# Four-image convolutional network on one core: the input of the tap matrices computed for two chunks of rows at a time, one on each half of TensorE's columns, with the second copy of each half written by VectorE

## The chip, the cores and the metric

The kernel runs on one core of one Trainium2 chip. The metric is the time of one execution on the device, in microseconds (us). Three runs before the change took 1929.0, 1927.67 and 1920.48 us, so the median is 1927.67 us. The profile comes from a further execution whose span is 1934.2 us; TensorE's granted clock was 0.961 of full speed on average in it.

## The reference

The input is a batch of 4 images of 256 channels and 56 x 56 pixels in fp32. Four residual layers follow each other, each on the group-normalised image:

- Layer 0 is an involution: a 1x1 convolution reduces the 256 channels to 64 (`h`), a second one makes from `h` 7 x 7 weights for each pixel and each of 16 groups of channels, and each pixel's 7 x 7 neighbourhood is summed with its own weights.
- Layer 1 is two 3x3 convolutions with batch norm and ReLU.
- Layer 2 is again an involution, with batch norm and ReLU after the first 1x1 convolution and after the sum.
- Layer 3 gates the image by channel and by pixel.

The change concerns the first 1x1 convolution of layers 0 and 2:

```python
h = jnp.einsum('bchw,oc->bohw', xk, reduce_w) + reduce_b[None, :, None, None]          # layer 0
t = jnp.einsum('bchw,oc->bohw', x, w1)
t = jax.nn.relu(_bn_eval(t, bn1_gamma, bn1_beta, bn1_mean, bn1_var))                    # layer 2
```

All is fp32 and stays so.

## The kernel before, in words

`involution_layer` handles layers 0 and 2, `conv_layer` layer 1; layer 3's gates are worked into layer 2. An involution layer goes through 8 units, one for each image `b` and block `cb` of 128 channels. A unit has two stages:

- `tap_matrices` (the tap stage): 32 steps of six matmuls (L436) that multiply `h` with shifted tables `z_sb`. Their results are brought from PSUM to `kt`, in three steps of four by VectorE (L454), in the fourth by ScalarE (L447).
- `apply`, over 7 columns `tx` of the image: 56 small matmuls (L478), of 64 columns and then of 32 columns of the array, multiply `kt` with the windows `xw` of the image. ScalarE (L491 in layer 0, L493 in layer 2) and VectorE (L498, in layer 2 also L505) take the results from PSUM. After the matmuls of each column come `next_windows`, which transposes a strip of the image (L364), copies it to `xw` (L365) and fills the rest of `xw` by DMA (L371, L373) for the column three places on, and `next_strip` (L345 or L347).

The 1x1 convolution is `bottleneck(b)`, a generator that is advanced step by step between other work. Its weights `red_sb` hold the 64 outputs twice, so that a matmul over all 128 columns of the array leaves `h` on partitions 0 to 63 and again on 64 to 127 of `hp`; `tap_matrices` reads both copies, one for each half of the array's rows. The first step scales the weights (`redn`, L384) and clears a corner of `hp` (L386, GpSimd), the second computes the bias `hb` (L391, L400 or L402). Seven further steps handle one chunk of 9 rows each (the last has 2 rows): two matmuls of 504 elements (L408), one for each block of input channels, then three ScalarE instructions (L420 in layer 0, L422 in layer 2) that write the chunk to `hp` in the order in which `tap_matrices` reads it.

All PSUM tiles of these layers come from one pool, `banks`, of four buffers of two banks, used in turn. `hp` has one buffer.

The order of the work is written out by hand: the main loop keeps lists `early[tx]` and `late[tx]` of steps that run ahead of a column's `apply` and after it, and at the end `in_order` ties each engine's instructions to the order in which the program wrote them. The first image's `bottleneck(0)` runs ahead of the first unit. That of image `b + 1` is spread over the columns of unit `(b, 1)`: in layer 0 the steps stand in `late[3]` to `late[5]` and `early[6]`, in layer 2 in `late[0]` to `late[5]` and `early[6]`.

## Time and profile before

| what | value |
|---|---|
| median of 3 runs | 1927.67 us |
| span of the profiled execution | 1934.2 us |
| TensorE busy | 1754.1 us, 91% |
| VectorE busy | 1413.4 us, 73% |
| ScalarE busy | 750.9 us, 39% |
| L408, matmuls of `bottleneck` | 224 records, 94.7 us |
| L478, matmuls of `apply` | 12544 records, 381.4 us |
| L436, matmuls of `tap_matrices` | 6144 records, 389.4 us |
| L454, VectorE's part of `kt` | 384 instructions, 357.6 us |

How to read it: the page names engines PE (TensorE matmuls), PEld (TensorE weight loads), DVE (VectorE), ACT (ScalarE), POOL (GpSimd) and SP (SyncE); a q behind an engine's name is its queue. A line such as L408 is a line of the kernel before. A group's row gives the tiles and shapes, the number of instructions, the time in which at least one of them ran, the mean duration of one, and the engine's idle time just before them with what ended it. Matmuls overlap, so a mean duration is longer than the pace at which they follow each other. The chain of work is followed back from the last instruction to what released it; a long share there means that the end waited for that line.

### The profile page before, as it was taken

To read this page: it belongs to the slowest core of one execution; us is meant where nothing else is said; L and a number is where in the kernel's file an instruction comes from. 1 tells how busy PE (TensorE), PEld (TensorE's weight loads), DVE (VectorE), ACT (ScalarE), POOL (GpSimd) and SP (SyncE) were. 2 spreads that over 40 slices of the span, in tenths; PEclk is the share of its full clock that TensorE was granted. 3 is DMA by queue.
4 is the path that set the end of the run, shared out by engine and by line. 5 is a ranking of instruction groups with operands and counts; after the bars stand their busy time and mean duration, and the time that the engine had idled before them with its cause. 6 is when DMAs were issued, how large, how long until landed. Compare 5 with 4: busy or idle time off the path is not lost.

```text
span 1934.2 us, 55654 instructions
## 1 busy us (share of the span) xinstructions
PE 1754.1 (91%) x24054; PEld 1535.3 (79%) x24054; DVE 1413.4 (73%) x2793; ACT 750.9 (39%) x1660; POOL 430.0 (22%) x615
## 2 busy tenths in 40 slices
PE   5999999999929999999999999997999899999876
PEld 4888888878828888988888888884887777878765
DVE  4685767856779978888887978864766666766773
ACT  2345445444422322222122222113656565565532
POOL 2233432334200000000000000000000581680672
PEclk9999999999969999989999999998999999999995
DMA  3544534444350201111111210113533763763651
GB/s 100 153 145 154 154 110 137 152 142 116 99 203 26 74 30 66 57 55 44 51 57 56 71 38 27 34 60 129 164 132 129 205 204 130 224 205 98 176 149 73
DMA packets 66964, 214.15 MB, mean 111 GB/s; under 512 B 13660, under 2 KB 21648, under 8 KB 63392
## 3 DMA queue, kind: packets, MB, share of 16 engines
q1 hardware_dynamic: 44526, 138.37, 22.9%
q0 software_dynamic: 14848, 65.85, 10.5%
q10 hardware_dynamic: 7346, 6.38, 1.1%
q8 instruction: 190, 3.11, 0.7%
q14 instruction: 54, 0.44, 0.1%
HBM read 74.68 MB, written 49.16 MB: 64 GB/s over the span
## 4 chain that ended last, share of the span: by engine, by line
PE 56%; DVE 30%; DMA 5%; issue 4%; POOL 3%; ACT 1%; SPq 1%; ACTq 0%; POOLq 0%; DVEq 0%
PE ps L478 15%; PE mm L1151 12%; DVE kt L454 12%; PE mm L1075 9%; PE ps L436 7%; PE ps L408 5%; PE ps L364 4%; DVE res L1144 3%; PE mm L1047 2%; DMA xw<-xw 2%; DVE un L498 1%; DVE v L1014 1%; PE ps L665 1%; DVE st L1194 1%; PE ps L561 1%
## 5 line engine op out<-in xcount | busy, mean ns | idle before, releaser
L478 PE MATMUL ps<-kt,xw 126*32 126x48 f32 (+1 forms) x12544 | 381.4, 235 | 41.6 <-issue 17.7
L478 PEld LDWEIGHTS ps<-kt,xw 126*32 126x32 f32 (+1 forms) x12544 | 339.8, 121 | 91.8 <-issue 48.8
L454 DVE TENSOR_TENSOR kt<-ps,zb_sb 126x798 f32<-126x798 f32 x384 | 357.6, 978 | 61.7 <-PE ps L436 61.0
L436 PE MATMUL ps<-hp,z_sb 64*126 64x133 f32 x6144 | 389.4, 283 | 12.1 <-DVE kt L454 6.2
L1151 PE MATMUL mm<-v,u_sb 128*128 128x280 f32 (+1 forms) x1728 | 392.6, 388 | 1.3 <-DVE u_sb L877 1.3
L436 PEld LDWEIGHTS ps<-hp,z_sb 64*126 64x126 f32 x6144 | 372.2, 189 | 26.5 <-DVE kt L454 7.4
L1151 PEld LDWEIGHTS mm<-v,u_sb 128*128 128x128 f32 x1728 | 331.0, 192 | 56.6 <-DVE u_sb L877 1.6
L447 ACT ACTIVATE kt<-ps,zb_sb 126x133 f32<-126x133 f32 x768 | 224.1, 441 | 173.4 <-PE ps L436 173.4
L1075 PE MATMUL mm<-v,u_sb 128*128 128x252 f32 (+1 forms) x864 | 192.3, 383 | 0.0
L498 DVE SCALAR_TENSOR_TENSOR un<-ps,par_sb,un 128x240 f32<-128x240 f32 x224 | 98.2, 457 | 123.8 <-ACT un L491 119.3
L498 DVE SCALAR_TENSOR_TENSOR un<-ps,s,un 128x240 f32<-128x240 f32 x224 | 102.4, 457 | 115.3 <-ACT un L493 109.4
L1075 PEld LDWEIGHTS mm<-v,u_sb 128*128 128x128 f32 x864 | 162.6, 189 | 26.1
L1188 POOL DMA_DIRECT2D x<-xr x24 | 13.1, 546 | 704.3 <-DVE xr L1187 704.3
L1047 PE MATMUL mm<-v,u_sb 128*128 128x126 f32 (+1 forms) x864 | 111.2, 281 | 39.2 <-ACT ph L950 30.0
L1047 PEld LDWEIGHTS mm<-v,u_sb 128*128 128x128 f32 x864 | 106.0, 194 | 41.8 <-issue 37.5
L503 POOL TENSOR_TENSOR xs<-un,xs 128x240 f32<-128x240 f32 x112 | 72.2, 664 | 225.5 <-DVE un L498 225.5
L365 ACT COPY xw<-ps 126x896 f32<-126x896 f32 x112 | 101.5, 906 | 48.0 <-PE ps L364 38.7
L1136 ACT ACTIVATE res<-xr,shift,norm_sb 128x1120 f32<-128x1120 f32 (+1 forms) x24 | 30.2, 1260 | 228.8 <-DVE xr L1187 156.2
L364 PE MATMUL ps<-ident_sb,strip_sb 128*126 128x128 f32 x784 | 111.6, 283 | 0.7 <-issue 0.6
L493 ACT ACTIVATE un<-ps,bn_t,s 128x240 f32<-128x240 f32 x112 | 60.2, 538 | 109.0 <-PE ps L478 105.5
L491 ACT ACTIVATE un<-ps,par_sb 128x240 f32<-128x240 f32 x112 | 50.2, 448 | 131.6 <-PE ps L478 129.8
L408 PE MATMUL ps<-xs,redn 128*128 128x504 f32 (+1 forms) x224 | 94.7, 570 | 4.5 <-DMA xs<-x 2.7
(173 smaller groups left out, 1950.8 us busy)
## 6 DMA issues: line engine op xcount, KB each, us to landing
xw<-xw SPq DMA_DIRECT2D x168, 252.0 KB
xw<-xw SPq DMA_DIRECT2D x224, 126.0 KB
xw<-xw POOLq DMA_DIRECT2D x56, 252.0 KB, 4.6
x<-xs POOLq DMA_DIRECT2D x8, 1568.0 KB, 7.8
xs<-in_x_dram SPq DMA_DIRECT2D x6, 1568.0 KB
xs<-x SPq DMA_DIRECT2D x6, 1568.0 KB
x<-xs SPq DMA_DIRECT2D x6, 1568.0 KB
gx<-x POOLq DMA_DIRECT2D x42, 224.0 KB, 6.3
```

The costliest lines, as they stand in the source:

```text
L364: nc.tensor.transpose(ps[:Q, k * P : (k + 1) * P], flat[:, k * Q : (k + 1) * Q], ident_sb)
L365: nc.scalar.copy(xw[:, :NSB, :], ps[:Q, : NSB * P].rearrange("q (n c) -> q n c", n=NSB))
L408: nc.tensor.matmul(ps[:, : rows * W], redn[:, ci].rearrange("p i r -> p (i r)"), xs_of[b, ci][:, j * ROWS_H * W : (j * ROWS_H + rows) * W] ...
L436: nc.tensor.matmul(ps[:Q, i, k * NT : (k + 1) * NT], z_sb[i * R : (i + 1) * R, cb * GB // 2 + gp, z0 : z0 + Q], hp[i * R : (i + 1) * R, py ...
L447: nc.scalar.activation(kt[:, g0 + i, pb, :, k], ps[:Q, i, k * NT : (k + 1) * NT], AF.Identity, bias=zb_sb[:, cb * GB + g0 + i, p0 + k : p0 ...
L454: nc.vector.tensor_tensor(kt[:, g0 : g0 + 2, pb], ps[:Q, :, : PB * NT].rearrange("q i (k t) -> q i t k", k=PB), zb_sb[:, cb * GB + g0 : cb ...
L478: nc.tensor.matmul(v[m * j : m * j + m, i, :, k * TP : (k + 1) * TP], xw[:, window(ty), m * j : m * j + m], kt[:, ng * j : ng * j + ng, :, ...
L498: nc.vector.scalar_tensor_tensor(part, o[e], s, part, ALU.mult, ALU.add)
L503: nc.gpsimd.tensor_tensor(dst, u, dst, ALU.add)
L1047: nc.tensor.matmul(ps[:, co * m : (co + 1) * m], u[ci][:, co * P : (co + 1) * P], v2[:, e, : n // 2, ci * WT : (ci + 1) * WT], start=(ci = ...
L1075: nc.tensor.matmul(ps, u1_sb[:, ci, dy, k, co * P : (co + 1) * P], v[:, k, dy * NB + ci : (dy + n - 1) * NB + ci + 1 : NB, :], start=(j == 0),
L1151: nc.tensor.matmul(ps, u2_sb[:, ci, dy, k, co * P : (co + 1) * P], v[:, k, dy * NB + ci : (dy + n - 1) * NB + ci + 1 : NB, :], start=(j == 0),
```

## The change

`bottleneck` takes two chunks of rows at a time. For each block of input channels it issues two matmuls, each with 64 of the 128 columns of `redn`: the first chunk goes to PSUM partitions 0 to 63, the second to 64 to 127 of one PSUM buffer. So each chunk's `h` comes out once and not twice. ScalarE writes each half to its own partitions of `hp`, with three instructions for each half. The other 64 partitions of each chunk are filled by a VectorE copy from `hp` to `hp` of 24 x 21 elements; the copies of one pair are issued in the step of the next pair, ahead of that step's ScalarE instructions. The layout of `hp` on each partition is as before. The seventh chunk, without a partner, is handled as before.

There are now four chunk steps and not seven, and the lists are adapted: in layer 0 the bias and two pairs run in `late[4]`, the third pair and the short chunk in `late[5]`, nothing in `early[6]`; in layer 2 the bias runs in `late[1]`, the pairs in `late[2]`, `late[3]` and `late[4]`, the short chunk in `late[5]`.

```diff
-                for j in range(NH):
-                    rows = min(ROWS_H, H - j * ROWS_H)
+                weights = [redn[:, ci].rearrange("p i r -> p (i r)") for ci in range(NB)]
+                copies = []
+                for j in range(0, NH, 2):
+                    halves = [slice(0, R), slice(R, P)] if j + 1 < NH else [slice(0, P)]
                     ps = one_bank()
                     for ci in range(NB):
-                        nc.tensor.matmul(
-                            ps[:, : rows * W],
-                            redn[:, ci].rearrange("p i r -> p (i r)"),
-                            xs_of[b, ci][:, j * ROWS_H * W : (j * ROWS_H + rows) * W],
-                            start=(ci == 0),
-                            stop=(ci == NB - 1),
-                        )
...
+                        for i, m in enumerate(halves):
+                            y0 = (j + i) * ROWS_H
+                            rows = min(ROWS_H, H - y0)
+                            nc.tensor.matmul(
+                                ps[m, : rows * W],
+                                weights[ci][:, m],
+                                xs_of[b, ci][:, y0 * W : (y0 + rows) * W],
+                                start=(ci == 0),
+                                stop=(ci == NB - 1),
+                            )
+                    for dst, part in copies:
+                        nc.vector.tensor_copy(dst, part)
+                    copies = []
...
+                    for i, m in enumerate(halves):
+                        rows = min(ROWS_H, H - (j + i) * ROWS_H)
+                        a0, n = (j + i) * ROWS_H // TY, -(-rows // TY)
+                        for py in range(min(rows, TY)):
+                            dst = hp[m, py, :, a0 : a0 + n, :]
+                            if layer == 0:
+                                nc.scalar.activation(dst, s[m, py, :, :n, :], AF.Identity, bias=hb[m])
...
+                        if len(halves) > 1:
+                            part = hp[:, :, :, a0 : a0 + n, :].rearrange("p y x a t -> p (y x) (a t)")
+                            copies.append((part[halves[1 - i]], part[m]))
                     yield
...
-                            late[4] += [step(g)] * 4
+                            late[4] += [step(g)] * 3
                             late[5] += [step(g)] * 3
-                            early[6] += [step(g)] * 2
...
                         late[0].append(step(g))
-                        late[1] += [step(g)] * 2
-                        for tx in range(2, 6):
+                        for tx in range(1, 6):
                             late[tx].append(step(g))
-                        early[6] += [step(g)] * 2
+                        early[6].append(step(g))
```

## The prediction

> **What bounds the kernel now.** I read the page first: the busy shares, then the chain of work that ended last.

> ```profile
> PE 1754.1 (91%) x24054; PEld 1535.3 (79%) x24054; DVE 1413.4 (73%) x2793; ACT 750.9 (39%) x1660; POOL 430.0 (22%) x615
> PE 56%; DVE 30%; DMA 5%; issue 4%; POOL 3%; ACT 1%; SPq 1%; ACTq 0%; POOLq 0%; DVEq 0%
> PE ps L478 15%; PE mm L1151 12%; DVE kt L454 12%; PE mm L1075 9%; PE ps L436 7%; PE ps L408 5%; PE ps L364 4%; DVE res L1144 3%; PE mm L1047 2%; DMA xw<-xw 2%; DVE un L498 1%; DVE v L1014 1%; PE ps L665 1%; DVE st L1194 1%; PE ps L561 1%
> ```

> PE is the bound over most of the span. The line that the change rewrites, L408 (the 1x1 convolution of `bottleneck`), holds 5% of the chain (4.6% where the chain is listed in full, 89 us), and its own busy time is 94.7 us: practically all of it is on the path. Next, the groups with their shapes kept apart, to see what a matmul on half the columns of the array costs here:

> ```profile
> L478 PE MATMUL ps<-kt,xw 126*64 126x96 f32 x4480 | 257.7, 266 | 31.9 <-DVE kt L454 16.0 <-issue 8.3 <-DMA xw<-xw 7.2
> ...
> L408 PE MATMUL ps<-xs,redn 128*128 128x504 f32 x192 | 91.2, 619 | 4.5 <-DMA xs<-x 2.7 <-DVE un L498 1.8
> ...
> L422 ACT ACTIVATE hp<-ps,hb,bn_s 128x168 f32<-128x168 f32 x72 | 30.2, 491 | 33.8 <-PE ps L408 33.8
> ...
> L420 ACT ACTIVATE hp<-ps,hb 128x168 f32<-128x168 f32 x72 | 23.7, 403 | 20.8 <-PE ps L408 20.8
> ```

> Each fp32 matmul leaves two records, its passes (96 matmuls of 504 elements are 192 records). Then the timeline of an image's `bottleneck` in layer 0 and, from the chain of waits over one stage of layer 2, the same work spread over columns:

> ```profile
> 154.94 5.31 PE L408 MATMUL ps<-xs,redn 128*128 128x504 f32 x12 [0.80 <-DVE un L498]
> ...
> 156.91 0.99 ACT L420 ACTIVATE hp<-ps,hb 128x168 f32<-128x168 f32 x3 [2.12 <-PE ps L408]
> ...
> 160.18 3.27 PE L478 MATMUL ps<-kt,xw 126*64 126x96 f32 x112
> ```

> ```profile
> 1425.75 3.22 PE ps L478 x108
> ...
> 1429.88 3.20 PE ps L478 x105
> ...
> 1434.34 1.86 PE ps L408 x4
> 1436.20 3.19 PE ps L478 x103
> ...
> 1440.31 1.69 PE ps L408 x4
> 1442.00 3.23 PE ps L478 x109
> ...
> 1457.75 3.81 PE ps L408 x12
> ```

> The reader is to see three things. A 504-element pass takes 0.422 us (the weight loads of 154.9 to 159.3 us follow one another at that pace; 1.69/4). A column without `bottleneck` takes 4.13 us, one with a chunk 5.82 us, so PE is the pace and the chunk adds its full time. And an image's 28 records cost 10.8 us of PE: 5.31 + 5.50 in layer 0, 1.86 + 3 x 1.69 + 3.81 = 10.74 in layer 2. For the first image of each layer nothing lies beside it:

> ```profile
> 24.12 11.39 PE L408 MATMUL ps<-xs,redn 128*128 128x504 f32 x26
> ...
> 38.18 2.32 PE L436 MATMUL ps<-hp,z_sb 64*126 64x133 f32 x36
> ```

> ```profile
> 1327.05 11.88 PE L408 MATMUL ps<-xs,redn 128*128 128x504 f32 x26 [2.70 <-DMA xs<-x]
> ...
> 1338.54 1.83 ACT L422 ACTIVATE hp<-ps,hb,bn_s 128x168 f32<-128x168 f32 x5 [0.43 <-PE ps L408]
> ...
> 1340.14 2.32 PE L436 MATMUL ps<-hp,z_sb 64*126 64x133 f32 x36 [1.21 <-ACT hp L422]
> ```

> [...] The trace agrees with the overlap: the 64-column group needs 257.7/4480 = 57.5 ns per record, where 96 elements at 0.422/504 us would be 80 ns alone and 40 ns in perfect pairs. [...]

> **The change, part by part.**

> *Matmuls.* Per image 12 long matmuls on 128 columns become 12 on 64 columns, two chunks side by side: 24 passes of 0.422 us (10.14 us) become 12 pair-passes. Perfect pairing gives 5.07 us. For the cost per pass I take L478's excess over perfect pairs, 57.5 - 40 = 17.5 ns a record, 35 ns a pair-pass: 12 x 0.457 = 5.48 us. So 4.66 to 5.07 us saved; I take 4.9. The seventh chunk stays as it was. The order of the matmuls (half 0, half 1, next channel block) alternates the tiles as L478 does. [...]

> *Evictions.* Six of 64 partitions per pair instead of three of 128 per chunk, with as many elements per partition: 20 per image before and after, 0.33 us each in layer 0 (0.99/3), 0.42 in layer 2 (30.2/72). No time saved there, but the pairs now arrive faster than ACT empties them.

> *Copies.* 6 per image, 48 in all, 504 elements. No row shows one[...]. I take 0.42 us: 20 us of DVE work. In the columns DVE does 1.8 us (four L498) and 0.6 us (L807), in layer 2 another 0.9 us (L505), of 4.1 to 5.8 us; 0.84 us fits. So 36 of the 48 cost nothing, hidden by L478[...].

> *Where a copy waits.* A copy waits for ACT, and the column's L498 are queued behind it on DVE; they free PSUM buffers for PE. In layer 2 the copies of a pair stand one column later: no wait. In layer 0 two pairs run in one burst. From its start at 0: the pairs end at 1.7 and 3.4 us; ACT evicts the first until 3.8, the second until 5.9; DVE copies the first by 4.7. The next column's L491 is ready at 3.4 + 2.0 = 5.4 us, so ACT delays it by 0.5 us, once per image, without stopping PE: the next user of its buffer in the ring of four runs some 4 us later. The last pair's copies wait until about 11.7 us and end by 12.5, where L498 is due at 12.6. Charge: 0 to 0.5 us per image.

> *Steps moved.* In layer 2 the pairs take columns 2 to 4 and the short chunk column 5; columns 2 to 4 keep 5.82 us, while 1, 5 and 6 get shorter. ACT then does L493 0.55 + 0.53, L365 0.91, L345 1.0 and six L422 2.5: 5.5 us of 5.82. Tight: L493 is delayed by up to 0.8 us, caught up within the column. No DMA is moved; SP and POOL keep their order.

> *Steady sum:* 3 images x 2 layers x 4.9 = 29.4 us.

> *First images.* Layer 0: PE ends near 31.3 instead of 35.4 us (the first passes run at half clock, 0.84 us), the bias matmuls (L298) at 34.1, the L305 copy on DVE at 35.2 (1.09 us), then three copies: L436 starts at 36.3 instead of 38.2. Gain 1.9 to 2.7 us, since L305 no longer stands behind L436; I take 2.3. Layer 2: pair ends near 1330.2, 1332 and 1333.7; ACT with 20 x 0.42 becomes the bound and ends the last pair at 1337, the copies follow at 1337.9 instead of 1340.1: 2.2 us.

> *Sum:* 29.4 + 2.3 + 2.2 = 33.9 us, less 1 us for ACT and DVE delays: 33 us. The profiled span is 1934.2 us, the median 1927.67 us (1920.48 to 1929.0); I subtract from the median: 1895 us. Less than 0.5% (about 10 us) could not be told from no change.

> **The rivals.**

> *A: another resource takes up the time in layer 2.* ACT at 95% in columns 2 to 4; and in its stages with gates (two of the three) a column without `bottleneck` already waits for windows: the chain has "DMA xw<-xw" pieces of 8.63 us at 1516.45, and columns of 6.1 us. If those two stages give back all (9.8 us) and ACT 0.5 us per column in nine (4.5 us): 1909 us. Against it: columns 2 to 4 keep their length, and windows are requested three columns ahead (12 us of slack left).

> *B: the halves do not overlap* on such long streams. Then PE keeps 10.8 us per image and only copies are added: about 2 us, for the first images: 1928 to 1932. Against it: 57.5 ns per record.

> *C, slower: the flush stops DVE.* Place: the copies ahead of L498 in the DVE queue. If each flush held PE by its whole wait, 1.7 + 2.0 + 0.8 = 4.5 us, 18 of them would cost 81 us and give 1976 us. It decides at 33/18 = 1.8 us per flush. [...] Against: 12 of 18 flushes (all of layer 2, the second of layer 0) find finished data; six wait, under other work.

> **How the numbers follow.** Forecast 0.77, A 0.11, B 0.06, C 0.06. The likeliest case alone spans 1887 to 1903 (4.66 or 5.07 us, first images 3 to 5.5 us, and a few us of scatter between runs). To hold 8 in 10 with A partly inside: 1886 to 1913. Faster 0.88 (forecast and A); within 0.5% 0.05 (most of B); slower 0.07 (C and the rest of B).

> **What would show it.** The L408 group falls from 94.7 to some 53 us busy; columns 2 to 4 in layer 2 keep 5.8 us, the burst of layer 0 falls from 5.31 + 5.50 to about 3.6 + 2.2 us; copies take 0.3 to 0.5 us; the chain holds none of them outside the first images. A shows as column 3 to 6 of layer 2 above 5.8 or 4.2 us, B as an unchanged L408 sum, C as PE idle before L478 or L364 released by DVE L498. I would be wrong if long streams on both halves slow each other, which L478's short ones would not tell.

## The result and the profile after

| | before | after |
|---|---|---|
| median of 4 runs each, on the same chip | 1928.34 us (1920.48 to 1932.41) | 1903.45 us (1899.0 to 1907.95) |
| span of the profiled execution | 1934.2 us | 1906.2 us |

The ratio is 0.9876, with a 95% interval of 0.9832 to 0.992: the kernel became faster by 24.9 us. 1895 us was forecast, with a range of 1886 to 1913.

In the changed kernel the lines shown before have moved: the matmuls of `bottleneck` are L416 (L408 before), those of `tap_matrices` L454 (L436), of `apply` L496 (L478). VectorE's part of `kt` is L472 (L454), its part of `un` L516 (L498). ScalarE's evictions are L433 and L435 (L420 and L422); the copies are L424. The page's busy shares and chain:

```profile
PE 1719.0 (90%) x24054; PEld 1516.7 (80%) x24054; DVE 1436.5 (75%) x2841; ACT 752.1 (39%) x1660; POOL 430.2 (23%) x615
PE 54%; DVE 29%; DMA 6%; issue 4%; POOL 3%; ACT 2%; SPq 1%; ACTq 0%; POOLq 0%; DVEq 0%
PE ps L496 14%; PE mm L1167 12%; DVE kt L472 10%; PE mm L1091 9%; PE ps L454 8%; PE ps L364 4%; DVE res L1160 3%; DMA xw<-xw 2%; PE mm L1063 2%; PE ps L416 2%; DVE un L516 2%; DVE v L1030 1%; PE ps L683 1%; DVE st L1210 1%; PE ps L579 1%
```

PE lost 35 us of busy time, DVE gained 23 us in 48 more instructions, and `bottleneck` fell from 5% of the chain to 2%. The groups with shapes kept apart (line, engine, operation, count, busy us and mean ns of one, idle time before them with what ended it):

```profile
L416 PE MATMUL ps<-xs,redn 128*64 128x504 f32 x192 | 50.9, 624 | 3.7 <-DMA xs<-x 2.3 <-DVE un L516 1.4
L424 DVE COPY hp<-hp 64x504 f32<-64x504 f32 x48 | 24.3, 506 | 27.6 <-ACT hp L433 14.2 <-ACT hp L435 13.0
L416 PE MATMUL ps<-xs,redn 128*128 128x112 f32 x32 | 5.3, 288 | 0.0
```

The number of records is the same 192, and a record is as long as before (624 ns against 619), but the group is busy for 50.9 us where it took 91.2: two records now run at a time. The timeline of PE in layer 2 has the same columns as the chain of waits shown before (start us, us, engine, line, operation, tiles, count, idle time before it):

```profile
1425.48 1.91 PE L416 MATMUL ps<-xs,redn 128*64 128x504 f32 x8
1427.22 3.24 PE L496 MATMUL ps<-kt,xw 126*64 126x96 f32 x112
...
1431.31 1.91 PE L416 MATMUL ps<-xs,redn 128*64 128x504 f32 x8
1433.05 3.20 PE L496 MATMUL ps<-kt,xw 126*64 126x96 f32 x112
...
1437.10 1.91 PE L416 MATMUL ps<-xs,redn 128*64 128x504 f32 x8
1438.84 3.21 PE L496 MATMUL ps<-kt,xw 126*64 126x96 f32 x112
...
1442.80 0.60 PE L416 MATMUL ps<-xs,redn 128*128 128x112 f32 x4
1443.80 3.25 PE L496 MATMUL ps<-kt,xw 126*64 126x96 f32 x112 [0.41 <-DVE un L516]
```

A column with a pair of chunks still goes at 5.8 us (1427.22, 1433.05, 1438.84), as a column with one chunk did before; there are three of them instead of four, and of the 3.81 us in which the last three chunks ran ahead of the seventh column only the short chunk's 0.60 us are left. The last line has the only idle time of PE there, 0.41 us.

In layer 0 two pairs run in one burst. The chain of waits over that stretch (start us, us, what):

```profile
154.47 3.67 PE ps L416 x16
158.13 3.08 PE ps L496 x100
161.21 0.92 PE ps L364 x7
162.13 2.47 PE ps L416 x12
164.59 3.24 PE ps L496 x111
```

Against 5.31 + 5.50 us it is 3.67 + 2.47 = 6.14 us, 4.67 us less for an image.

To see what reached the end, I took from both traces the time from the first to the last `apply` matmul of each of the six stages that hold a later image's `bottleneck`:

| stage | before, us | after, us | gain |
|---|---|---|---|
| layer 0, images 1, 2, 3 | 42.6, 42.0, 43.0 | 37.4, 37.0, 38.3 | 5.2, 5.0, 4.7 |
| layer 2, image 1 (no gates beside it) | 40.5 | 35.7 | 4.8 |
| layer 2, images 2 and 3 (gates beside them) | 40.5, 40.6 | 36.6, 36.8 | 3.9, 3.8 |

Together 27.4 us, from one trace of each kernel.

The first image of each layer is another story. The timeline of the changed kernel in layer 0 (all engines, other lines left out), and then in layer 2:

```profile
30.94 3.21 PE L298 MATMUL ps<-ident_sb,xs 16*126 16x16 f32 x48
34.19 1.09 DVE L305 COPY zb_sb<-ps 126x384 f32<-126x384 f32 x1 [3.73 <-PE ps L298]
35.31 1.32 DVE L424 COPY hp<-hp 64x504 f32<-64x504 f32 x3
36.78 3.88 PE L454 MATMUL ps<-hp,z_sb 64*126 64x133 f32 x36 [2.63 <-DVE hp L424]
```

```profile
1316.21 8.33 ACT L435 ACTIVATE hp<-ps,hb,bn_s 64x168 f32<-64x168 f32 x20 [29.20 <-PE ps L416]
1323.86 0.42 DVE L424 COPY hp<-hp 64x504 f32<-64x504 f32 x1 [0.86 <-ACT hp L435]
1324.43 4.36 PE L454 MATMUL ps<-hp,z_sb 64*126 64x133 f32 x36 [4.29 <-DVE hp L424]
```

Before, the same 36 records of the tap matmuls took 2.32 us in both layers; now 3.88 and 4.36 us. PE waits 2.63 and 4.29 us for ScalarE and the copies, and then runs slowly. The view by windows shows why (window, its us, PE busy us and records, granted clock, DMA share, GB/s), first of the kernel after and then of the kernel before:

```profile
1320.20:1324.40 4.20, 0.00 (x0) 0.89 0.01 2
1324.50:1328.70 4.20, 4.20 (x36) 0.50 0.01 4
```

```profile
1340.20:1342.40 2.20, 2.20 (x37) 1.00 0.05 11
```

Behind the wait in layer 2 the granted clock is half. In layer 0 too, but there it fell before PE began to wait at 34.15 us, as the windows of the kernel after show:

```profile
29.80:33.21 3.41, 3.41 (x48) 1.00 0.00 0
33.21:36.62 3.41, 0.94 (x10) 0.50 0.00 0
36.63:40.03 3.40, 3.25 (x29) 0.50 0.02 5
```

PE is busy all through the first of these, two thirds of it (2.27 us) with the small bias matmuls of 16 x 16 elements (L298). There are 24 of them, with two records each: the 48 and 96 "small matmuls" of the expectations below are records. "Busy" means that record follows record; the ends of matmuls in a trace are modelled, so short pauses inside would not show. What the small matmuls have to do with the clock was first an open question.

So although the tap stage starts earlier, its first results don't come earlier. From a common mark (the second group-mean matmul L199 in layer 0, the clearing of the strip L326 in layer 2) the first tap matmul comes at 16.0 instead of 16.81 us in layer 0 and at 26.24 instead of 28.08 us in layer 2, but the first `apply` matmul at 51.81 instead of 51.15 us and at 55.58 instead of 54.63 us.

### The profile page after: what moved, and what is told of

Its sections match the earlier page's. It is cut to its first block, busy times and chain, and to the rows that moved or that the text cites. A ratio compares the mean times of both kernels' runs of the same rounds, so it can differ in the third digit from the quotient of the medians.

```text
span 1906.2 us, 55688 instructions
## 1 busy us (share of the span) xinstructions
PE 1719.0 (90%) x24054; PEld 1516.7 (80%) x24054; DVE 1436.5 (75%) x2841; ACT 752.1 (39%) x1660; POOL 430.2 (23%) x615
## 4 chain that ended last, share of the span: by engine, by line
PE 54%; DVE 29%; DMA 6%; issue 4%; POOL 3%; ACT 2%; SPq 1%; ACTq 0%; POOLq 0%; DVEq 0%
PE ps L496 14%; PE mm L1167 12%; DVE kt L472 10%; PE mm L1091 9%; PE ps L454 8%; PE ps L364 4%; DVE res L1160 3%; DMA xw<-xw 2%; PE mm L1063 2%; PE ps L416 2%; DVE un L516 2%; DVE v L1030 1%; PE ps L683 1%; DVE st L1210 1%; PE ps L579 1%
## 5 line engine op out<-in xcount | busy, mean ns | idle before, releaser
L496 PE MATMUL ps<-kt,xw 126*32 126x48 f32 (+1 forms) x12544 | 380.2, 235 | 43.7 <-issue 17.2
L496 PEld LDWEIGHTS ps<-kt,xw 126*32 126x32 f32 (+1 forms) x12544 | 340.5, 121 | 89.5 <-issue 50.4
L454 PE MATMUL ps<-hp,z_sb 64*126 64x133 f32 x6144 | 390.7, 283 | 18.2 <-DVE hp L424 7.2
L454 PEld LDWEIGHTS ps<-hp,z_sb 64*126 64x126 f32 x6144 | 372.6, 189 | 33.6 <-issue 8.6
L472 DVE TENSOR_TENSOR kt<-ps,zb_sb 126x798 f32<-126x798 f32 x384 | 357.8, 979 | 46.9 <-PE ps L454 46.1
L516 DVE SCALAR_TENSOR_TENSOR un<-ps,s,un 128x240 f32<-128x240 f32 x224 | 102.5, 458 | 95.8 <-ACT un L511 91.9
L516 DVE SCALAR_TENSOR_TENSOR un<-ps,par_sb,un 128x240 f32<-128x240 f32 x224 | 98.2, 457 | 87.4 <-ACT un L509 83.1
L1063 PEld LDWEIGHTS mm<-v,u_sb 128*128 128x128 f32 x864 | 107.3, 196 | 41.6 <-issue 37.4
L365 ACT COPY xw<-ps 126x896 f32<-126x896 f32 x112 | 101.5, 906 | 48.6 <-PE ps L364 36.8
L1152 ACT ACTIVATE res<-xr,shift,norm_sb 128x1120 f32<-128x1120 f32 (+1 forms) x24 | 30.2, 1259 | 227.7 <-DVE xr L1203 156.2
L364 PE MATMUL ps<-ident_sb,strip_sb 128*126 128x128 f32 x784 | 112.4, 284 | 0.1
L130 POOL TENSOR_TENSOR norm_sb<-norm_sb,mhalf 128x1 f32<-128x1 f32 x32 | 17.8, 557 | 335.9 <-DVE norm_sb L129 330.3
```

The costliest lines, as they stand in the source:

```text
L364: nc.tensor.transpose(ps[:Q, k * P : (k + 1) * P], flat[:, k * Q : (k + 1) * Q], ident_sb)
L365: nc.scalar.copy(xw[:, :NSB, :], ps[:Q, : NSB * P].rearrange("q (n c) -> q n c", n=NSB))
L454: nc.tensor.matmul(ps[:Q, i, k * NT : (k + 1) * NT], z_sb[i * R : (i + 1) * R, cb * GB // 2 + gp, z0 : z0 + Q], hp[i * R : (i + 1) * R, py ...
L472: nc.vector.tensor_tensor(kt[:, g0 : g0 + 2, pb], ps[:Q, :, : PB * NT].rearrange("q i (k t) -> q i t k", k=PB), zb_sb[:, cb * GB + g0 : cb ...
L496: nc.tensor.matmul(v[m * j : m * j + m, i, :, k * TP : (k + 1) * TP], xw[:, window(ty), m * j : m * j + m], kt[:, ng * j : ng * j + ng, :, ...
L516: nc.vector.scalar_tensor_tensor(part, o[e], s, part, ALU.mult, ALU.add)
```

## The experiments

The theory after this result: (1) the two halves run beside each other, and that is the whole gain; (2) ScalarE at 95% and the copies cost next to nothing in the later images; (3) the first images gain nothing since PE's wait costs it the clock. The rivals are those of the prediction; and for (3), that something other than the wait lowers the clock.

**Both chunks on the same half.** All else is kept, the 64-column matmuls and the copies too; the second chunk goes to the same PSUM partitions in a second bank.

```diff
-                    halves = [slice(0, R), slice(R, P)] if j + 1 < NH else [slice(0, P)]
-                    ps = one_bank()
+                    halves = [slice(0, R), slice(0, R)] if j + 1 < NH else [slice(0, P)]
+                    ps = two_banks()
...
-                                ps[m, : rows * W],
+                                ps[m, i, : rows * W],
...
-                            copies.append((part[halves[1 - i]], part[m]))
+                            copies.append((part[R:P], part[m]))
```

> Both chunks of a pair go to the same 64 columns of the array, one after the other (two banks of one PSUM buffer), and all copies go from partitions 0-63 to 64-127; everything else is as in the changed kernel. Theory (the gain is the overlap of the two halves): a pair takes 3.4 us of PE again instead of 1.84 us, the 504-element matmuls are some 85 to 91 us busy instead of 50.9 us, and the time goes back to 1925 to 1938 us. Rival (the gain is in narrower matmuls, fewer steps or their new places): a pair stays near 1.84 us and the time near 1903 us.

It took 1926.57 us against 1927.18 for the kernel before, ratio 0.9999 (0.9986 to 1.0012). Its group of long matmuls:

```profile
L416 PE MATMUL ps<-xs,redn 128*64 128x504 f32 x192 | 90.9, 623 | 3.5 <-DVE un L516 2.5 <-DMA xs<-x 1.0
```

90.9 us busy, as in the kernel before (91.2), though each matmul fills only half of the columns. The six stages of the table take 42.6, 42.1, 43.0, 40.4, 40.4 and 40.5 us, as before the change. Fewer columns saved no time by themselves, and fewer steps didn't either: the gain in these stages is that the halves overlap. The equal times alone would say less. In this trace the first `apply` comes 3.4 us (layer 0) and 2.4 us (layer 2) later after the marks than in the kernel before, so something like 6 us must have been gained elsewhere; where is not shown.

**Half by half.** Does it matter that neighbours in the program alternate between the halves, as the prediction assumed?

```diff
-                    for ci in range(NB):
-                        for i, m in enumerate(halves):
+                    for i, m in enumerate(halves):
+                        for ci in range(NB):
```

> The two loops are swapped: both channel blocks of the first half, then both of the second half, still on different columns of the array. If each half takes its matmuls from a queue of its own that runs ahead, a pair stays at 1.84 us, the 504-element group at about 51 us and the time at 1898 to 1908 us. If matmuls start in program order and only neighbours can run together, at most the last matmul of the first half and the first of the second overlap: a pair takes 2.5 to 3.0 us, the group 70 to 82 us busy, and the time is 1912 to 1925 us.

1905.54 us in one run, and in groups and timeline:

```profile
L416 PE MATMUL ps<-xs,redn 128*64 128x504 f32 x192 | 51.6, 640 | 4.8 <-DMA xs<-x 2.8 <-DVE un L516 1.2 <-ACT xw L365 0.8
```

```profile
1426.79 1.92 PE L416 MATMUL ps<-xs,redn 128*64 128x504 f32 x8
```

A pair takes 1.92 us, in the same view of the changed kernel 1.91. So the first half's four records didn't hold back those of the second, which stand behind them in the program.

**PE kept busy.** Some 504-element matmuls that multiply an image with the identity are put ahead of the first tap stage of each layer, three in layer 0 and four in layer 2; nobody reads their results.

```diff
+            def keep_busy(n):
+                ps = one_bank()
+                for _ in range(n):
+                    nc.tensor.matmul(ps[:, : ROWS_H * W], ident_sb, xs_of[0, 0][:, : ROWS_H * W], start=True, stop=True)
...
                 run(make_tables(z_sb, zb_sb, span, sb, scratch, nc.scalar))
+                keep_busy(3)
...
                 run(bottleneck(0))
+                keep_busy(4)
```

> As the changed kernel, with matmuls that nobody reads in the wait before the first tap stage of each layer: three of 504 elements in layer 0 (2.5 us), four in layer 2 (3.4 us). Theory (TensorE waits 2.6 and 4.3 us there for ScalarE and the copies, falls to half clock and gives back what the first images had gained): the first 36 tap matmul records take 2.3 us instead of 3.88 us in layer 0 and 4.36 us in layer 2, the first column of the first unit starts 1.5 us earlier in layer 0 and 2 to 3 us earlier after the start of layer 2; the time falls by some 4 us to 1897 to 1902 us (inside the scatter of single runs, so the windows decide). Rival (they are slow for another reason, say the copies' late arrival or PSUM): 3.9 and 4.4 us as before, nothing gained.

One run took 1910.26 us. The timeline of PE (the fillers are L246, the tap matmuls L459, the small bias matmuls L303):

```profile
32.28 2.81 PE L303 MATMUL ps<-ident_sb,xs 16*126 16x16 f32 x48
35.03 4.50 PE L246 MATMUL ps<-xs,ident_sb 128*128 128x504 f32 x6
39.46 2.32 PE L459 MATMUL ps<-hp,z_sb 64*126 64x133 f32 x36
...
1322.43 3.56 PE L246 MATMUL ps<-xs,ident_sb 128*128 128x504 f32 x8
1326.48 2.32 PE L459 MATMUL ps<-hp,z_sb 64*126 64x133 f32 x36 [0.49 <-DVE hp L429]
```

The 36 records are back at 2.32 us in both layers, and in layer 2 the first `apply` comes at 52.62 us from the mark, 2.96 us sooner than in the changed kernel. That settles the cause there. In layer 0 it came 0.9 us later (52.73): the fillers themselves took 4.50 us for six records, where 0.422 us each would be 2.5, and the tap matmuls queued behind them. The windows of this kernel:

```profile
32.30:35.00 2.70, 2.70 (x49) 1.00 0.00 0
35.50:38.90 3.40, 3.40 (x5) 0.50 0.02 5
39.50:41.70 2.20, 2.20 (x37) 1.00 0.00 0
```

The clock fell behind the 48 records of 16 x 16 elements although PE had no idle time, so in layer 0 the wait was not, or not alone, the cause. The single time, above that of the changed kernel, is not explained by these two places, which add up to a gain of 2 us. A part of the difference comes from layer 1, which no kernel here changes and which alone took between 775.6 and 783.1 us in the runs.

**Copies twice.** Each copy is issued twice. If the flush stops DVE and PE with it, that must double.

```diff
                     for dst, part in copies:
                         nc.vector.tensor_copy(dst, part)
+                        nc.vector.tensor_copy(dst, part)
```

> Each of the 48 copies is made twice. Theory (in the six later images the copies are hidden by the matmuls of apply): columns 1 to 6 of the units with a bottleneck keep their length within 0.2 us, only the first images' tap stages start 0.4 to 1.3 us later: 1903 to 1907 us. Rival (the flush of the copies holds VectorE and through PSUM TensorE): 18 flushes by 0.84 us or more: 15 us more, 1917 us or above.

1902.98 us in one run. The groups:

```profile
L424 DVE COPY hp<-hp 64x504 f32<-64x504 f32 x48 | 23.4, 487 | 20.1 <-ACT hp L436 10.5 <-ACT hp L434 8.3
L425 DVE COPY hp<-hp 64x504 f32<-64x504 f32 x48 | 27.7, 577 | 1.6
```

27.7 us of DVE work were added, and the four stages without gates keep their length: 37.6, 37.0, 38.3 and 35.7 us against 37.4, 37.0, 38.3 and 35.7. A trace is left behind them: the tap stages that follow in layer 0, which are DVE's, take 0.9 us more each (25.9, 25.7 and 25.7 against 25.0, 24.8 and 24.8). The two stages with gates were 1.6 and 0.9 us longer, within their own scatter (below). Rival C falls.

**First image as before.** For `b == 0` the old loop over seven chunks on all 128 columns is put back; the later images use pairs.

```diff
+                if b == 0:
+                    for j in range(NH):
...
+                    return
                 weights = [redn[:, ci].rearrange("p i r -> p (i r)") for ci in range(NB)]
```

> The first image of layers 0 and 2 uses the matmuls of before (128 columns, no copies), the other six images the pairs. Theory (the first images lose more to the half clock than the pairs save): after its start (the second group-mean matmul in layer 0, the clearing of the strip in layer 2) the first column comes at about +51.2 us in layer 0 and +54.6 us in layer 2, as in the kernel before, instead of +51.8 and +55.6 us in the changed kernel; its first 36 tap records take 2.3 us; 1.6 us gained in all. Rival (the pairs save time there too and the loss lies elsewhere, in layer 1 say): the first columns come 2 us later than in the changed kernel.

1902.93 us in one run. The first `apply` comes at 50.48 us (layer 0) and 54.59 us (layer 2) from the marks, the 36 records take 2.32 us again. So PE that works longer gets there no later than PE that waits: the pairs are worth nothing in the first images, or less than nothing by about 1 us.

**Pairs spread out.** In layer 2 the pairs stand in columns 1, 3 and 5 instead of 2, 3 and 4, so that ScalarE has a column to catch up after each.

```diff
-                        for tx in range(1, 6):
-                            late[tx].append(step(g))
-                        early[6].append(step(g))
+                        late[1] += [step(g)] * 2
+                        late[3].append(step(g))
+                        late[5].append(step(g))
+                        early[6] += [step(g)] * 2
```

> In layer 2 the three pairs run after columns 1, 3 and 5 and the short chunk ahead of column 6, instead of after 2, 3, 4 and 5. If ScalarE, 95% full in three columns in a row, costs time, the units with a bottleneck (35.7, 36.6 and 36.8 us from their first matmul of apply to their last in the changed kernel) get shorter by 1 us each. If it is the window DMAs of the two units with gates, only those two change, by up to 1 us either way. If neither, all stay within 0.3 us. Time 1899 to 1906 us.

The three stages took 35.6, 36.5 and 37.0 us against 35.7, 36.6 and 36.8. ScalarE's crowded columns cost nothing that this can measure, though PE's wait of 0.41 us is gone. The single time was 1913.79 us, above the 1899 to 1906 us expected. Part of its excess stands in layer 0, where the first `apply` came at 54.99 us, with three windows of 3.4 us at half clock in a row.

**Combined, and the changed kernel again.** The first image of layer 0 as before, four fillers in layer 2 (results nobody reads), the pairs spread; beside it the changed kernel itself, six runs each.

> The pairs for all images but the first of layer 0, which is as before; matmuls that nobody reads in the wait of layer 2's first image (four of 504 elements); the pairs of layer 2 after columns 1, 3 and 5. Theory: 0.6 us better in layer 0 and 3 us in layer 2 than the changed kernel, whose own ratio is near 0.987: a ratio of 0.984 to 0.986. Rival (the waits only move): the ratio of the changed kernel, 0.987 to 0.989.

> The changed kernel once more, unaltered, on the same chip and in the same rounds as the combined kernel, to tell a difference of 3 us: ratio 0.986 to 0.989, 1901 to 1906 us.

The combination took 1900.47 us (1897.86 to 1908.96), ratio 0.9873 (0.9853 to 0.9893); the changed kernel 1902.07 us (1894.36 to 1908.88), ratio 0.9885 (0.9865 to 0.9905). The first images did what they should, at 50.94 and 52.93 us from the marks, but the intervals overlap: a version faster than the changed kernel is not shown.

**The small matmuls.** The last two runs ask what lowers the clock in layer 0. Take the windows of 3.4 us, ahead of the first tap stage of layer 0, in which the small matmuls ran and PE had no gap: over the runs so far the clock had been halved behind each that held 2.0 us or more of them, and behind none that held 1.8 us or less. (The expectation below leaves out that PE had no gap. With a wait in the window less was enough: in the changed kernel's repetition the window from 32.55 us held 1.10 us of small matmuls and no other work of PE, and the next one was at half clock.) The first kernel handles the first images as before, so that PE doesn't wait, and issues each of the 24 small matmuls twice:

```diff
-                    nc.tensor.matmul(
+                    for _ in range(times):
+                        nc.tensor.matmul(
...
-                run(make_tables(z_sb, zb_sb, span, sb, scratch, nc.scalar))
+                run(make_tables(z_sb, zb_sb, span, sb, scratch, nc.scalar, times=2))
```

> The first image is handled as in the kernel before (all 128 columns, no copies), so that TensorE has no wait ahead of the first tap matmuls in layer 0; each of the 48 small bias matmuls (16 x 16) there is issued twice, the second time with the same result. If TensorE's clock falls only after idle time, the granted clock stays at 1.00 from the long matmuls on, the 96 small ones take about 5.6 us, the 36 tap records 2.32 us, and the first apply matmul comes about 2.8 us later than with 48 (some 53.7 us from the second group-mean matmul). If windows of 3.4 us that are mostly filled by such small matmuls count as idle (in the runs so far the clock was halved behind every window with 2.0 us or more of them, and behind none with 1.8 us or less), at least one window must be granted half the clock although TensorE is never idle, and the 36 tap records or the second half of the small matmuls take up to twice as long.

The timeline of PE, and its windows:

```profile
36.17 8.39 PE L299 MATMUL ps<-ident_sb,xs 16*126 16x16 f32 x96
44.48 4.33 PE L477 MATMUL ps<-hp,z_sb 64*126 64x133 f32 x36
```

```profile
35.00:38.40 3.40, 3.40 (x47) 1.00 0.00 0
38.42:41.82 3.40, 3.40 (x37) 0.50 0.02 5
41.83:45.23 3.40, 3.40 (x32) 0.50 0.00 0
45.24:48.64 3.40, 3.40 (x34) 0.50 0.00 0
```

PE is busy without a gap, and three windows are at half clock. The 96 records take 8.39 us and not 5.6, the 36 tap records 4.33 us, and the first `apply` comes at 59.18 us. Here small matmuls, 2.23 us of them in the window from 35.00 us, were enough to lower the clock without a wait of PE. (The run as a whole took 1921.63 us.)

The traces show it at a second place, too, where nothing was changed: the tables of layer 2 are made with 48 such records at about 60 us. In the kernel before they fill 2.71 us of the window from 61.12 to 64.53 us, in which PE has no gap and the clock is 1.00, and the next window is at 0.50. In ten of the other eleven traces one window holds 2.5 to 2.8 us of them, with the same outcome; in the eleventh the clock was already half. What it is about these matmuls, their size, the few rows and columns they use or pauses that the records hide, is not shown.

The second kernel is the kept-busy one, with more fillers between the small matmuls. Three were meant, but `p` runs from 0 to 23, so two are issued:

```diff
+                    if fill and p in (11, 23, 35):
+                        keep_busy(1)
```

> As the kept-busy kernel (three filler matmuls ahead of the first tap stage of layer 0, four in layer 2, results that nobody reads), but in layer 0 one more filler of 504 elements is put after the 12th, 24th and 36th of the 48 small bias matmuls, so that no window of 3.4 us holds more than about 1.6 us of small ones. If the small ones count as idle, the clock now stays at 1.00 and the fillers behind them run at 0.422 us a record (the kept-busy kernel: 0.5 and 0.75 us a record). If it was something else in that place (the wait of VectorE, the phase of the windows), the clock is half behind the small matmuls here too. The first apply of layer 0 isn't expected sooner than in the kept-busy kernel, since the table copy on VectorE waits for the longer row of matmuls.

The kernel missed its aim: in the trace all five fillers, ten records, stand behind the 48 small records (35.19 to 42.7 us), so no window was diluted. The clock was halved behind a window with 2.3 us of small ones, as in the other runs, and the first fillers followed each other at 0.84 us a record. The first `apply` came at 55.06 us, the run took 1900.56 us. That dilution would keep the clock up is not shown.

## Why the prediction was right, and which of its terms was off

*Overlap: right, in mechanism and size.* The prediction gave a pair 4 x 0.457 = 1.83 us, from the short matmuls' 57.5 ns a record; the chain shows 1.84 us. The burst of layer 0 was forecast at 3.6 + 2.2 us and is 3.67 + 2.47. The group's busy time was forecast at 53 us and is 56.2 (50.9 + 5.3), from 94.7. PE's own time for an image fell by 4.67 us in layer 0, the price from L478 (4.66). The four stages without gates became shorter by 4.9 us on average, as forecast, though where the 0.2 us beyond PE's own time come from is not shown; the two with gates gave 3.9 and 3.8 us, and this is why the six gave 27.4 us instead of 29.4. The run with both chunks on one half takes away the overlap alone: the six stages went back to their old length. The overlap that rival B denied is there, and makes the gain.

*Copies: right but for one place.* The shortest took 416 ns, the median 420; 0.42 us had been the author's estimate, from no trace, so that the exact hit is luck. But ten of the 48 took 0.59 to 1.43 us, and each of these lies beside a GpSimd instruction. The timeline of DVE in a stage of layer 2 with gates, then of POOL, and two pieces of the chain:

```profile
1573.63 0.85 DVE L424 COPY hp<-hp 64x504 f32<-64x504 f32 x2
...
1579.67 2.71 DVE L424 COPY hp<-hp 64x504 f32<-64x504 f32 x2
```

```profile
1573.77 1.13 POOL L668 TENSOR_SCALAR gx<-gx,gscale,gbias 128x448 f32<-128x448 f32 x1
...
1578.99 0.73 POOL L668 TENSOR_SCALAR gx<-gx,gscale,gbias 128x448 f32<-128x448 f32 x1
1579.68 1.15 POOL L669 TENSOR_TENSOR gn<-gn,sfb 128x448 f32<-128x448 f32 x1
1580.90 1.20 POOL L670 TENSOR_TENSOR gx<-gx,gn 128x448 f32<-128x448 f32 x1
```

```profile
1579.67 1.43 DVE hp L424
1581.12 1.27 DVE hp L424
```

The pair of copies at 1573.63 us began before GpSimd's instruction and took 0.42 us each, and that instruction took 1.13 us, where one of the same line took 0.73 at 1578.99. The pair at 1579.67 us met GpSimd already at work and took 2.71 us. So the one that comes second seems to pay. Once it was GpSimd, by 0.40 us (1.13 against 0.73), once the two copies, by 1.87 us (2.71 against 0.84); the prediction had priced nothing for it. These two copies are the only ones on the chain outside the first images, where the prediction said there would be none: 2.7 us on it where 0.84 were forecast. By how much that lengthened the stage, the scatter between the runs hides.

*Waits of the flush: right.* Up to 0.5 us for an image was charged and "without stopping PE" said. Doubling the copies left the four ungated stages as they were, so rival C had no place to act. ScalarE's crowding in layer 2 was also judged rightly: "delayed by up to 0.8 us, caught up within the column" became one PE wait of 0.41 us, and spreading the pairs out changed no stage by more than 0.2 us. Of rival A that part falls. Its other part, the stages with gates, has something for it. They gave 3.9 and 3.8 us where the ungated stage of the same layer gave 4.8, and over the nine traces of kernels with pairs there (all but that with doubled copies) 3.2 and 2.7 us on average, where the ungated one gave 4.8 again. But they moved between 35.9 and 40.3 us in these traces with the same work in them; the cause of that is not shown.

*First images: wrong.* The step "*First images*" took 2.3 us in layer 0 and 2.2 us in layer 2 as gains. It saw how far the tap stage's start would move (forecast: 1.9 and 2.2 us sooner; measured from the marks: 0.8 and 1.84), and took that for the gain. What it left out is the clock. In the clock records of the traces of both kernels every stretch at one granted clock, but for the last, lasts a whole multiple of 3.41 us, and the windows of 3.4 us in this document are those. In each of the changed kernel's first images two of them are at 0.50 (33.21 to 40.04 us in layer 0, 1323.45 to 1330.28 us in layer 2), and the next is at 1.00 again. A wait did not have to fill a window. In the first tap stage of layer 0 every one of the twelve traces has a wait of PE of 2.23 to 2.25 us; in the kernel before the window around it, 54.29 to 57.71 us, holds 1.17 us of PE's work, and the next window is at 0.50, as in the other eleven.

In layer 2 the wait is the cause. In the six kernels that wait for copies there and have no fillers PE stood for 2.13 to 4.32 us and the clock fell; in the other six, with fillers or the old loop, it stood for 1.21 us at most and the clock stayed at 1.00. In layer 0 two things come together: the small bias matmuls, which in the run with twice as many were followed by three windows at 0.50 without a wait of PE, and the wait of 2.63 us that follows them. With the old loop the 48 small records, 2.81 us in all, had full work on both sides, and in all three traces an edge of the windows fell among them, so that no window got 2.0 us of them (1.78 us in the kernel before) and the clock stayed up. That is in part luck: in the kept-busy kernel they also had full work on both sides, all 2.81 us fell into one window, and the clock was halved.

How much this cost in layer 0 went with the number of windows at half clock, whose edges lay differently from run to run (one at 33.21 us in the changed kernel, at 32.55 us in its repetition, at 33.84 us with the pairs spread): with one window at half clock the first `apply` came at 50.76 us (the changed kernel's repetition), with two at 51.81 and 52.14, with three at 54.99. Over the five runs of pairs without fillers (one with its copies doubled) it came at 52.6 us on average, over the three runs of the old loop with 48 small records at 50.9 (50.48 to 51.15). In layer 2 the five came at 55.2 us on average (54.25 to 55.88), the three kernels with the old loop at 54.63, 54.59 and 54.42. So the gains of 2.3 and 2.2 us did not arrive; that the pairs lose time there is likely, but rests on few traces.

*Sum.* -27.4 us in the six stages, 52.6 - 50.9 = +1.7 in layer 0's first image and 55.2 - 54.6 = +0.6 in layer 2's make -25.1 us; the medians differ by 24.9. So close an agreement is luck: with the nine traces' average in the stages, -25.4 us, it would be -23.1. The forecast had subtracted 33 us. Of the miss of 8 us, 6.8 are the first images (a gain of 4.5 that became a loss of 2.3) and 2 the stages with gates, less the 1 us that had been charged for delays. The time lies within the range of 1886 to 1913 us since the large term, the overlap, was right and the range was wide. It lies just above the likeliest part, 1887 to 1903 us, which had been built on first images that gain 3 to 5.5 us. The profiled spans differ by 28.0 us; with layer 1 alone scattering by 7 us from run to run, a single span could not have settled it.

*What stays open.* What makes the stages with gates scatter, and whether the 1.6 and 2.1 us that they gave less on average are lost or come back in the stages around them. What it is about the small matmuls that lowers the clock. And how often the old loop would meet the half clock in layer 0, which three traces can't tell.

## What to carry to other kernels

Two matmuls that each needed 64 of the 128 columns ran side by side here, at 0.46 us a pair of 504-element records against 0.422 us for one alone, and a row of the same kernel that already did so gave the price (0.457 us). When a change takes work from PE, look at what PE waits for next, and at the granted clock there: ahead of the PE-bound stages of the first images a wait of 2.13 us or more, or a window with 2.0 us or more of tiny matmuls, was followed by a clock of 0.50, and the earlier start was lost again. In the stages without gates, where other matmuls filled PE's time, all of the saving arrived, 4.9 us an image; beside the gates it was less.
